# A sparse four-layer graph network on one core: layer 3 gathers only filled slots, shorter clears behind fourth gathers, and layer 2 moved inside the layer 1 loop

## The chip, the cores and the metric

The kernel runs on one core of a Trainium2 chip. The metric is the time of one execution in microseconds on the device. Of several executions the median is given. The trace and its page come from one further execution, taken by the hardware profiler. TensorE is PE in the profile (its weight loads are PEld), VectorE is DVE, ScalarE is ACT, GpSimd is POOL and SyncE is SP.

## The reference

The input is x, 2708 rows of 128 floats, and adj, a 2708 x 2708 matrix. adj has random entries with a density of 0.0059 and a full diagonal, so a row holds some 17 entries, and at most 32. Four layers follow each other, each as `x = layernorm(x + layer(x, adj))`:

```python
# layer 0: mean over the incoming entries
adj.T @ x / adj.sum(axis=0)
# layer 1: messages, an update, its own layer norm
messages = gelu(s[:, None, :] + d[None, :, :] + msg_b)      # s, d: two projections of x
aggregated = einsum('ijd,ij->id', messages, adj)
h = gelu(concat([x, aggregated]) @ upd_w.T + upd_b) + x
# layer 2: batch norm over the rows, leaky ReLU
h = adj @ (x @ W) + b
# layer 3: four heads of attention over the neighbours
s = leaky_relu(x1[:, None, :] + x2[None, :, :], 0.01) @ a    # x1 = x @ w1, x2 = x @ w2
s = exp(tanh(s / 8) * 8) * adj
out = leaky_relu(s / s.sum(-1, keepdims=True) @ x @ Wlin.T, 0.01)
concat(out of the heads) @ w
```

Only pairs (i, j) with an entry in adj matter in layers 1 and 3. The kernel has a sparse path, described here, for inputs whose rows have few enough entries, and a dense one, which this input doesn't take. Arrays named `wrong`, `wrong3` collect whether an input breaks an assumption of the sparse path.

## The kernel before

**Layer 0.** The rows of adj are loaded in 22 blocks of 128 rows. For each block TensorE adds up layer 0's product (L453), GpSimd clears the diagonal (an affine_select, L443), and VectorE extracts the entries of each row, column numbers and values, into lists of 32 slots (`extract`; max8 and find_index, L483 and L478). The nodes are sorted by their number of entries, in two groups: the first 13 blocks and the other 9 (`SPLIT = 13`). Sorted rows lie in 22 new blocks; `QUARTERS` states for every 32 rows of a block how many slots can be filled at most. A tile `caps` holds those limits, written by 88 GpSimd memsets of 32x1 at the start (L415); VectorE uses it in layer 0's checks. After layer 0 the table `d_dram` holds a row d for every node, and `dx_dram` what a node needs for itself.

**Layers 1 and 2** run together. A loop goes over i = 0..21 with the sorted block b = TURNS[i]. `messages` (L919) transposes the block's x into a PSUM tile `own`, computes its term s with two matmuls (the second adds msg_b), and then takes the neighbours in chunks of 5 to 8 slots, 55 chunks in all. For each slot GpSimd gathers up to 128 rows of `d_dram` with one indirect DMA (L263) into a chunk tile `msg`; there are five chunk tiles, used in turn. VectorE adds s (L954), ScalarE applies GELU (L957), VectorE weighs each slot and adds it up (L938). `update` (L964) computes the new x of the block, and SyncE writes it to `x2_dram`, which the profile calls x_dram (digits are left out of names); x2_first and x2_second appear as x_first and x_second. With the last chunks some blocks of layer 3's lists are spread over partitions (`spread`, L669 and L675). Each iteration then also transposes a block of adj's rows (`transposed`, TensorE L1029, ScalarE L1034, SyncE L1036) into `at_dram`.

For layer 2, `layer2(k)` (L1061) gathers 128 whole rows of `at_dram` into `at_rows` (1.4 MB) and multiplies them with x @ W into six PSUM banks (L1076, six matmuls of up to 512 columns). From i = 11 on each iteration calls `layer2` for two values of k at its end. From i = 14 on each iteration also gathers two blocks of the first group's x back in the original order (`x2_first`, 13 gathers).

All gathers of d_dram, t2_dram and x2_dram go through `gather_spaced` (L272). After every fourth gather of a table it clears a tile `pause` of 200 bytes three times (L280), ordered behind the gather; the next gather of that table is ordered behind the last clear.

The order of instructions on each engine in these layers is not written by hand. A scheduler sorts what the program lists, by dependencies and estimated durations. So a change in the program can move instructions far from its own line, on several engines; the built order of each engine is known before any run.

**Between layers 2 and 3** come the batch norm, the masks for the seven kinds of layer 3 blocks (`masks`, L1165: which slot and row a partition stands for), and a table `t2_dram` with a row of 644 floats per node: its projection for four heads (512), its x (128) and four terms of the heads.

**Layer 3** is ordered by hand. The sorted nodes lie in 24 blocks (`BLOCKS3`), each of four quarters of g x j rows. A chunk holds g rows with c = 128 // g slots each on g x c partitions (120 to 128). Four chunks, one of each quarter, make a quad; there are 100 quads. `fetch(i)` (L1635) gathers the four chunks of a quad into a tile `g4` (a pool of `GOT = 9`). `repeated` (L1455) lets TensorE repeat the own terms for the slots (L1463) and add chunks 2 and 3 of g4 (L1469). VectorE adds z to chunks 0 and 1 in place (L1663) and computes leaky ReLU times a for the others (L1664, L1479) and for chunks 0 and 1 (L1487), writing the products into g4 over the gathered projections. ScalarE sums them per head (L1495). `rest` (L1499) takes two quads at a time: tanh, exp, the softmax sum (L1519), and the weighted sum of neighbours with TensorE (L1540), which reads another part of g4. `finish` and the layer norm follow per block, and an indirect DMA scatters finished rows to the output (L284). In the loop the gathers of quad i + 1 are issued at the start of quad i, as far as free tiles allow.

## Time and profile before

| what | value |
|---|---|
| median of 3 runs | 1655.01 us (1653.0 to 1659.47) |
| profiled execution | 1660.39 us, span 1658.7 us |
| mean granted TensorE clock | 0.755 |
| busy share of PE / DVE / ACT / POOL | 70% / 66% / 49% / 63% |
| L263 POOL, gathers of t2_dram (layer 3) | 400, 400.0 us busy, mean 1000 ns |
| L263 POOL, gathers of d_dram (layer 1) | 368, 347.9 us busy, mean 945 ns |
| L280 POOL, clears of pause | 591, 150.5 us busy, mean 255 ns |
| layer 0 / layers 1 and 2 / between / layer 3 and end | 0 to 207 / 207 to 864 / 864 to 959 / 959 to 1659 us |

The span runs from the first to the last instruction of the profiled execution; the difference to its time is what the device needs around it. In lines of the profile `g<-t_dram,idx` names what is written and what is read, `x400` is the number of instructions, and `<-` ahead of an engine or DMA names what ended an idle time. The time that GpSimd is shown in an indirect DMA counts as busy (L263); issuing any other DMA doesn't. "issue" as a releaser means that the engine waited for nothing that the profile shows.

### The profile page before, as it was taken

To read this page: it belongs to the slowest core of one execution; us is meant where nothing else is said; L and a number is where in the kernel's file an instruction comes from. 1 tells how busy PE (TensorE), PEld (TensorE's weight loads), DVE (VectorE), ACT (ScalarE), POOL (GpSimd) and SP (SyncE) were. 2 spreads that over 40 slices of the span, in tenths; PEclk is the share of its full clock that TensorE was granted. 3 is DMA by queue.
4 is the path that set the end of the run, shared out by engine and by line. 5 is a ranking of instruction groups with operands and counts; after the bars stand their busy time and mean duration, and the time that the engine had idled before them with its cause. 6 is when DMAs were issued, how large, how long until landed. Compare 5 with 4: busy or idle time off the path is not lost. (4 is left out here: it accounts for less than half of the span.)

```text
span 1658.7 us, 23258 instructions
## 1 busy us (share of the span) xinstructions
PE 1164.1 (70%) x5179; PEld 735.5 (44%) x5179; DVE 1093.4 (66%) x4560; ACT 811.9 (49%) x3491; POOL 1045.7 (63%) x1656
## 2 busy tenths in 40 slices
PE   7976434566248667353576778988889788898985
PEld 6976323445136433131333324544444445454444
DVE  6999767888435452264465555877768777587874
ACT  2638467755134210021122545776658666576763
POOL 2001487777776626777762577777777777777772
PEclk9998555555555578676566877999889999788996
DMA  8633367879546744811111576777677676676761
GB/s 277 260 135 132 90 171 226 240 213 259 135 103 174 252 172 153 314 52 48 41 42 35 202 204 189 200 212 204 190 202 219 192 199 187 191 208 188 216 190 39
DMA packets 163651, 288.42 MB, mean 174 GB/s; under 512 B 46786, under 2 KB 118514, under 8 KB 156401
## 3 DMA queue, kind: packets, MB, share of 16 engines
q0 software_dynamic: 60208, 189.68, 39.4%
q1 hardware_dynamic: 98053, 93.97, 18.4%
q10 hardware_dynamic: 5240, 3.18, 0.8%
q8 instruction: 44, 0.72, 0.2%
q14 instruction: 106, 0.87, 0.2%
HBM read 241.22 MB, written 45.45 MB: 173 GB/s over the span
## 5 line engine op out<-in xcount | busy, mean ns | idle before, releaser
L263 POOL DMA_INDIRECT g<-t_dram,idx x400 | 400.0, 1000 | 149.0 <-issue 105.7
L263 POOL DMA_INDIRECT msg<-d_dram,idx x368 | 347.9, 945 | 132.6 <-issue 78.7
L1495 ACT ACTIVATE g<-g 126x128 f32<-126x128 f32 (+3 forms) x1200 | 352.9, 297 | 65.7 <-DVE g L1487 25.7
L1469 PE MATMUL z<-g,ident 126*126 126x512 f32 (+3 forms) x400 | 245.4, 734 | 69.6 <-DMA g<-t_dram,idx 60.2
L1495 ACT ACTIVATION_READ_ACCUMULATOR g<-g 126x1 f32 (+3 forms) x1200 | 226.0, 188 | 3.6 <-issue 3.3
L1029 PE MATMUL pt_a<-ident,rows 128*128 128x128 f32 (+2 forms) x475 | 119.5, 411 | 118.8 <-ACT at_sb L1034 62.4
L1469 PEld LDWEIGHTS z<-g,ident 126*126 126x126 f32 (+3 forms) x400 | 73.8, 213 | 229.0 <-DMA g<-t_dram,idx 151.7
L1463 PE MATMUL z<-x,copies 32*126 32x512 f32 (+3 forms) x800 | 160.8, 686 | 7.8 <-DVE g L1663 4.8
L280 POOL MEMSET pause<- 1x200 int8 x591 | 150.5, 255 | 20.7
L453 PE MATMUL acc<-x_nat,rows 128*128 128x129 f32 (+3 forms) x1012 | 132.2, 293 | 30.5 <-DMA rows<-in_adj_dram 19.4
L1029 PEld LDWEIGHTS pt_a<-ident,rows 128*128 128x128 f32 (+2 forms) x475 | 84.4, 210 | 146.8 <-ACT at_sb L1034 76.1
L1663 DVE TENSOR_TENSOR g<-g,z 126x1024 f32<-126x1024 f32 (+3 forms) x100 | 121.7, 1217 | 41.8 <-PE z L1463 21.5
L1076 PE MATMUL acc<-at_rows,x_nat 128*128 128x512 f32 (+2 forms) x264 | 139.4, 676 | 13.4 <-DMA at_rows<-at_dram,perm 13.4
L453 PEld LDWEIGHTS acc<-x_nat,rows 128*128 128x128 f32 (+2 forms) x1012 | 126.1, 202 | 36.2 <-DMA rows<-in_adj_dram 20.7
L1487 DVE SCALAR_TENSOR_TENSOR g<-g,a_ps 126x1024 f32<-126x1024 f32 (+3 forms) x100 | 121.2, 1212 | 0.0
L938 DVE SCALAR_TENSOR_TENSOR own<-msg,ls,own 128x128 f32<-128x128 f32 (+1 forms) x302 | 105.4, 349 | 20.6 <-ACT msg L957 10.5
L957 ACT ACTIVATE msg<-msg 128x896 f32<-128x896 f32 (+4 forms) x55 | 50.4, 916 | 137.7 <-DVE msg L954 68.6
L1479 DVE SCALAR_TENSOR_TENSOR g<-z,a 126x128 f32<-126x128 f32 (+3 forms) x400 | 91.9, 285 | 35.0 <-PE z L1469 31.0
L1540 PEld LDWEIGHTS po_s<-wm,g 126*128 126x128 f32 (+3 forms) x800 | 105.3, 208 | 17.4 <-issue 12.3
L954 DVE TENSOR_TENSOR msg<-msg,own 128x896 f32<-128x896 f32 (+4 forms) x55 | 57.4, 1043 | 79.8 <-DMA msg<-d_dram,idx 76.1
L1540 PE MATMUL po_s<-wm,g 126*128 126x24 f32 (+6 forms) x800 | 103.4, 280 | 1.4 <-DVE wm L1527 0.9
L478 DVE FIND_INDEX8 ci<-cv,rows 128x8 uint32<-128x247 f32 (+2 forms) x242 | 98.5, 407 | 0.0
(319 smaller groups left out, 2058.2 us busy)
## 6 DMA issues: line engine op xcount, KB each, us to landing
rows<-in_adj_dram SPq DMA_DIRECT2D x34, 1354.0 KB
at_dram<-at_sb SPq DMA_DIRECT2D x105, 256.0 KB
t_dram<-t_row SPq DMA_DIRECT2D x10, 644.0 KB
g<-t_dram,idx POOLq DMA_INDIRECT x400
msg<-d_dram,idx POOLq DMA_INDIRECT x368
x_s<-dx_dram SPq DMA_DIRECT2D x21, 128.0 KB
at_dram<-at_sb SPq DMA_DIRECT2D x21, 64.0 KB
x_dram<-x_n SPq DMA_DIRECT2D x21, 64.0 KB
```

Of the source, the lines that this page charges most:

```text
L263: return nc.gpsimd.indirect_dma_start(out=dst, out_offset=None, in_=table[0 : min(N, table.shape[0]), :], in_offset=bass.IndirectOffsetOnA ...
L280: did = nc.gpsimd.memset(pause, 0)
L453: nc.tensor.matmul(accs0[k][0:m, c0 : c0 + f1 - f0], lhsT=rows[0:n, j0 : j0 + m], rhs=x_nat[0:n, b, f0:f1], start=k not in started, stop=( ...
L938: nc.vector.scalar_tensor_tensor(to, m, v, last, ALU.mult, ALU.add)
L1029: nc.tensor.transpose(pt[0:m, j, 0:n], rows[0:n, c0 : c0 + m], ident[0:n, 0:n])
L1076: nc.tensor.matmul(accs2[c][:, 0:cw], lhsT=xw[0:n, b, :], rhs=at[0:n, c0 : c0 + cw], start=(k == 0), stop=(k == NBLK - 1),)
L1463: nc.tensor.matmul(z2[0:e, r, :] if r < 2 else zs[r - 2][0:e], lhsT=copies[g][rows, j, :], rhs=own[b][1][rows, :], start=True, stop=r < 2, ...
L1469: nc.tensor.matmul(zs[r - 2][0:e], lhsT=ident[0:e, 0:e], rhs=g4[0:e, r, 0:HD], start=False, stop=True, skip_group_check=True,)
L1487: nc.vector.scalar_tensor_tensor(z, z, 0.0, a_ps[0:e].unsqueeze(1).to_broadcast((e, 2, HD)), ALU.max, ALU.mult)
L1495: nc.scalar.activation(product, product, AF.Identity, accum_out=sc[0:e, r, hd : hd + 1])
L1540: nc.tensor.matmul(po[:, p0 * HEADS : (p0 + g) * HEADS], lhsT=g4s[i][0:e, r, HD : HD + D], rhs=wm[0:e, 4 * i + r, :, :], start=True, stop= ...
L1663: nc.vector.tensor_tensor(z, z, z2[0:e], ALU.add)
```

## The change

- `gather_spaced` clears `pause` twice after a fourth gather instead of three times (394 clears in all instead of 591).
- Layer 3 lays its slots out slot by slot (c, g) instead of row by row (g, c), so that filled slots come first, and a new table `QUARTERS3` states how many slots a quarter of a block fills. From the ninth quad on a gather fetches only `g * QUARTERS3` rows. The first eight quads fetch all rows, which leaves finite numbers in all eight tiles. Rows gathered in layer 3: 50,460 before, 47,208 after. The new counts are 128 (60 gathers), 126 (61), 120 (70), 119 (32), 117 (21), 115 (16), 114 (40), 112 (36), 110 (32), 108 (9), 105 (5), 104 (3), 100 (3), 96 (6) and 90 (6).
- `GOT` is 8, and the g4 tiles are eight fixed ones. The results of VectorE go to a new tile `made` (two buffers) instead of into g4.
- `masks` builds the mask of a row from an iota over all c x g slots, a comparison and a reduction, instead of from an iota over g.
- `wrong3` has two columns per block; `caps3` and `of_block` serve the new check of the counts.
- The memsets of `caps`, now with those of `caps3`, stand behind the first rows of adj instead of at the start: 126 instead of 88, of them 46 of 128x1 and 80 of 32x1.
- `layer2(k)` is called in `messages`, behind the matmul that adds msg_b (`term`), for two values of k in each iteration from i = 12 on, and one iteration later than before. In the built order of TensorE, k = 5 to 13 stood between the own transposes of iterations 13 and 14 before; after it there are two blocks in each of the iterations 12 to 21.
- `x2_first` is gathered from i = 16 on, three blocks in each iteration. In the built order of GpSimd its first gather stood behind the fourth gather of chunk 34 before, and stands behind the sixth gather of chunk 36 after (chunks counted from 0).

```diff
+QUARTERS3 = [
+    (31, 26, 25, 24), (23, 22, 22, 22), (21, 21, 21, 20), (20, 20, 20, 19),
+    (19, 19, 19, 19), (18, 18, 18, 18), (18, 17, 17, 17), (17, 17, 16, 16),
+    (16, 16, 16, 16), (15, 15, 15, 15), (14, 14, 14, 14), (14, 13, 13, 13),
+    (13, 12, 12, 12), (11, 11, 10, 9), (30, 26, 24, 24), (23, 23, 22, 21),
+    (21, 21, 20, 20), (20, 19, 19, 19), (18, 18, 18, 18), (17, 17, 17, 16),
+    (16, 16, 16, 15), (15, 15, 14, 14), (14, 13, 13, 13), (12, 12, 11, 9),
+]
...
-GOT = 9
+GOT = 8
...
-    wrong3 = keep.tile([P, NB3], FP, name="wrong3")
+    wrong3 = keep.tile([P, 2 * NB3], FP, name="wrong3")
...
-            for _ in range(3):
+            for _ in range(2):
...
-        for b in range(NBLK):
-            for q, most in enumerate(QUARTERS[b]):
-                nc.gpsimd.memset(caps[32 * q : 32 * q + 32, b : b + 1], float(most))
+        caps3 = work.tile([P, NB3], FP, name="caps3")
...
-                part = mine.tile([P, g, c], FP, name=f"spread{g}", tag="spread", bufs=2)
+                part = mine.tile([P, c, g], FP, name=f"spread{g}", tag="spread", bufs=2)
                 nc.vector.tensor_tensor(
                     part,
-                    lists3[:, b % 6, k0 : k0 + c].unsqueeze(1).to_broadcast((P, g, c)),
-                    of_row[g].unsqueeze(2).to_broadcast((P, g, c)),
+                    lists3[:, b % 6, k0 : k0 + c].unsqueeze(2).to_broadcast((P, c, g)),
+                    of_row[g].unsqueeze(1).to_broadcast((P, c, g)),
                     ALU.mult,
                 )
                 nc.tensor.matmul(
                     po[0:e, c0 + i * q : c0 + (i + 1) * q],
-                    lhsT=part.rearrange("p g c -> p (g c)"),
+                    lhsT=part.rearrange("p c g -> p (c g)"),
...
-            n, bad = 4 * g * j, wrong3[:, b : b + 1]
-            nc.vector.tensor_scalar(bad[0:n], node3[0:n, b, 0:1], float(c - 1), None, ALU.is_gt)
+            n = 4 * g * j
+            nc.vector.tensor_scalar(
+                wrong3[0:n, b : b + 1], node3[0:n, b, 0:1], 1.0, None, ALU.is_lt
+            )
             nc.vector.scalar_tensor_tensor(
-                bad[0:n], node3[0:n, b, 0:1], 1.0, bad[0:n], ALU.is_lt, ALU.add
+                wrong3[:, NB3 + b : NB3 + b + 1], lists3[:, b % 6, 2 * SLOTS : 2 * SLOTS + 1],
+                caps3[:, b : b + 1], of_block[g * j], ALU.is_gt, ALU.mult,
...
-        of_row, of_chunk = {}, {}
+        of_row, of_chunk, of_block = {}, {}, {}
+        spans = sorted({g * j for g, j in BLOCKS3})
+        of_blocks3 = work.tile([P, len(spans)], FP, name="of_blocks3")
+        for i, e in enumerate(spans):
+            of_block[e] = of_blocks3[:, i : i + 1]
+            nc.vector.tensor_scalar(of_block[e], in32, float(e), None, ALU.is_lt)
...
+        for b in range(NBLK):
+            for q, most in enumerate(QUARTERS[b]):
+                if not q or most != QUARTERS[b][0]:
+                    at = slice(32 * q, 32 * q + 32) if q else slice(0, P)
+                    nc.gpsimd.memset(caps[at, b : b + 1], float(most))
+        for b in range(NB3):
+            for q, most in enumerate(QUARTERS3[b]):
+                if not q or most != QUARTERS3[b][0]:
+                    at = slice(32 * q, 32 * q + 32) if q else slice(0, P)
+                    nc.gpsimd.memset(caps3[at, b : b + 1], float(most - 1))
...
-        def messages(b, x_s, three):
+        def messages(b, x_s, three, beside):
...
-            nc.tensor.matmul(
+            term = nc.tensor.matmul(
                 s_ps[0:n], lhsT=ones[0:1, 0:n], rhs=msgb[0:1, :], start=False, stop=True
             )
+            for k in beside:
+                with tc.issue_after(term.ins):
+                    layer2(k)
...
-            x_st, agg = messages(b, x_s, three)
+            x_st, agg = messages(
+                b, x_s, three,
+                range(2 * (i - 12), 2 * (i - 11) if i + 1 < NBLK else i) if i > 11 else (),
+            )
...
-            if i >= 11:
-                for k in range(2 * (i - 11), min(i, 2 * (i - 10))):
-                    layer2(k)
-            if i > SPLIT:
-                if i == SPLIT + 1:
+            if i > SPLIT + 2:
+                if i == SPLIT + 3:
                     x2_first = late.tile([P, SPLIT, D], FP, name="x2_first", tag="late")
-                for b in range(2 * (i - SPLIT - 1), min(SPLIT, 2 * (i - SPLIT))):
+                for b in range(3 * (i - SPLIT - 3), min(SPLIT, 3 * (i - SPLIT - 2))):
...
-            nc.gpsimd.iota(row_of, pattern=[[1, g], [0, c]], base=0, channel_multiplier=0)
-            start = small.tile([P, g], I32, name=f"start{g}", tag="start", bufs=2)
-            nc.gpsimd.iota(start, pattern=[[-c, g]], base=0, channel_multiplier=1)
+            nc.gpsimd.iota(row_of, pattern=[[0, c], [1, g]], base=0, channel_multiplier=0)
+            apart = small.tile([P, c, g], I32, name=f"apart{g}", tag="apart", bufs=2)
+            nc.gpsimd.iota(apart, pattern=[[-g, c], [-1, g]], base=0, channel_multiplier=1)
...
-            after = small.tile([P, g], FP, name=f"after{g}", tag="after", bufs=2)
+            here = small.tile([P, c, g], FP, name=f"here{g}", tag="here", bufs=2)
+            nc.vector.tensor_scalar(
+                here.rearrange("p c g -> p (c g)"), apart.rearrange("p c g -> p (c g)"),
+                0.0, None, ALU.is_equal,
+            )
+            mask[g] = ready.tile([P, g], FP, name=f"mask{g}")
+            nc.vector.tensor_reduce(mask[g], here.rearrange("p c g -> p g c"), AX.X, ALU.add)
             count = small.tile([P, 1], FP, name="count", bufs=2)
-            nc.vector.tensor_scalar(
-                after, start, 0.0, None, ALU.is_ge, ALU.add, accum_out=count
-            )
-            mask[g] = ready.tile([P, g], FP, name=f"mask{g}")
             nc.vector.scalar_tensor_tensor(
-                mask[g], start, float(c), after, ALU.is_lt, ALU.mult
+                each, jrow[:, 0:g], 1.0, mask[g], ALU.add, ALU.mult, accum_out=count
...
-        got = layer.enter_context(tc.tile_pool(name="s3_got", bufs=GOT, reuse_waits="tile"))
+        got = layer.enter_context(tc.tile_pool(name="s3_got", bufs=1, reuse_waits="tile"))
...
-        def products(e, g4):
-
-            z = g4[0:e, 0:2, 0:HD]
+        def products(e, made):
+
+            z = made[0:e, 0:2, :]
...
+        sets = [got.tile([P, 4, RW], FP, name=f"g4_{i}") for i in range(GOT)]
+
         def fetch(i):
             b, j = quads[i]
             e = BLOCKS3[b][0] * (P // BLOCKS3[b][0])
-            g4 = got.tile([P, 4, RW], FP, name="g4")
+            g4 = sets[i % GOT]
             for r in range(4):
                 ch = CHUNK3[b] + 4 * j + r
-                gather_spaced(g4[0:e, r, :], t2_dram, idx3[0:e, ch : ch + 1])
+                m = BLOCKS3[b][0] * QUARTERS3[b][r] if i >= GOT else e
+                gather_spaced(g4[0:m, r, :], t2_dram, idx3[0:m, ch : ch + 1])
...
-            z, a_row = g4[0:e, 0:2, 0:HD], a_99.rearrange("p h d -> p (h d)")
-            nc.vector.tensor_tensor(z, z, z2[0:e], ALU.add)
+            made = small.tile([P, 4, HD], FP, name="made", bufs=2)
+            a_row = a_99.rearrange("p h d -> p (h d)")
+            nc.vector.tensor_tensor(made[0:e, 0:2, :], g4[0:e, 0:2, 0:HD], z2[0:e], ALU.add)
             nc.vector.scalar_tensor_tensor(
-                g4[0:e, 2, 0:HD], zs[0][0:e], 0.0, a_row[0:e], ALU.max, ALU.mult
-            )
-            scores(e, 3, zs[1], a_row, g4, sc4[:, 3, :])
+                made[0:e, 2, :], zs[0][0:e], 0.0, a_row[0:e], ALU.max, ALU.mult
+            )
+            scores(e, 3, zs[1], a_row, made, sc4[:, 3, :])
```

## The prediction

> **What bounds the kernel now.** I read the page's engine rows first: no engine is over 70% busy, so the bound changes along the way. The windows view, cut at the stages, says where (columns: stretch, its length, then busy us and instructions of PE, PE's weight loads, DVE, ACT and POOL, the granted clock, the DMA share, GB/s):
>
> ```profile
> 207.00:443.00 236.00, 120.92 (x505) 92.62 (x504) 173.72 (x866) 139.11 (x253) 180.14 (x272) 0.54 0.78 216
> 443.00:592.00 149.00, 81.63 (x292) 59.38 (x292) 69.68 (x355) 45.51 (x116) 104.77 (x156) 0.53 0.63 183
> 592.00:629.00 37.00, 34.57 (x113) 19.46 (x114) 21.66 (x104) 8.07 (x25) 0.87 (x3) 0.85 0.19 69
> 629.00:864.00 235.00, 121.67 (x347) 67.84 (x346) 102.38 (x408) 36.31 (x93) 180.30 (x273) 0.68 0.35 115
> ...
> 959.00:1620.00 661.00, 574.52 (x2583) 308.16 (x2586) 480.82 (x1582) 436.08 (x2672) 493.57 (x716) 0.89 0.71 201
> ```
>
> In four of the five POOL is the busiest or near it, and its idle time there is made of the 0.30 us that follows every gather: 716 instructions in layer 3, 400 of them gathers with 0.30 behind each, fill 661 us. Second, POOL's own timeline. It shows a quad of layer 3, and the one long hole:
>
> ```profile
> 592.35 0.25 POOL L280 MEMSET pause<- 1x200 int8 x1
> 628.74 0.95 POOL L263 DMA_INDIRECT x_first<-x_dram,rank  x1 [36.13 <-issue]
> ...
> 1028.28 1.19 POOL L263 DMA_INDIRECT g<-t_dram,idx  x1 [0.30 <-issue]
> ...
> 1253.24 0.95 POOL L263 DMA_INDIRECT g<-t_dram,idx  x1 [0.30 <-issue]
> ...
> 1337.46 0.88 POOL L280 MEMSET pause<- 1x200 int8 x3
> 1338.94 1.00 POOL L263 DMA_INDIRECT g<-t_dram,idx  x1 [0.60 <-ACT lin_s L1566]
> ```
>
> Four gathers and three clears repeat with no other hole: 99 quad periods from 959.0 to 1615.0, 6.63 us each. The hole at 592.6 is the first gather of x2_first; it needs the rows that update 12 writes, whose write SyncE issued at 626.40. Third, the waits view, for who waits on whom:
>
> ```profile
> PEld z L1469 <- DMA g<-t_dram,idx: 151.7, 116, 4.6
> ...
> POOL x_first L263 <- issue: 38.1, 13, 36.1
> ```
>
> In layer 3 TensorE waits for gathered rows; POOL waits for TensorE only 8.7 + 6.2 us (what released L263 in the groups view). So **POOL bounds layer 3**, and layers 1 and 2 except from 443 to 629. There DVE's add L954 starts 20 to 51 us after its chunk's gathers ended, all five chunk tiles are full, and the chain of DVE, ACT, TensorE and the loads of dx_dram sets the pace.
>
> **Part 1, one clear fewer behind a fourth gather.** Three clears show as 0.88 us, two as 0.57 elsewhere in the timeline: 0.31 less, 100 times in layer 3, **-31 us**. The transfers had it as cover if they need the pause; against that, the first eight quads (128 rows, cheapest) ran at 5.75 us a quad and 224 GB/s without a wait of POOL, faster than the ~6.3 expected here. In layers 1 and 2 there are 97 clears fewer: 30 us of POOL, worth something only where POOL is the bound.
>
> **Part 2, rows of empty slots.** 50,460 rows of layer 3 become 47,208. Rows are not what POOL pays for: by the timeline a 128-row gather takes 0.947, 126 rows 0.984, 120 rows 0.980, 125 rows 1.197; in layer 1, 96 rows 0.932 and 32 rows 0.882. After the change 102 gathers have a count that 16 divides, 224 another even count, 74 an odd one. By the rows nearest: 102 x 0.947 + 224 x 0.982 + 74 x 1.197 = 405 us, against 400.0 now: **+5**. Bounds for the 209 gathers whose count has no row in layer 3: all at 0.932 gives -18, all at 1.197 gives +37. What the rows save lies in the DMA engines (71% busy, not the bound), so I count nothing for it.
>
> The 125-row gather costs 0.21 more than the 126-row one, though it moves less. The Trainium skill, page "DMA: Bandwidth & Descriptors", section "Why a DMA increments its semaphore by 16 and not by 1", has a rule for it: a DMA uses the largest number of engines up to 16 that divides the row count. That speaks against this change, since 128 rows use 16 engines, but 119 use 7, 117 use 13, 115 use 5 and 114 use 6. A line through the 126- and 125-row durations (9 against 25 rows per engine) makes the sum +2.5 instead of +5 by this estimate; 115 and 119 rows would then be the dear ones, 117 would not, and the time 1583.
>
> The g4 tiles are 8 instead of 9 and results go to `made`. In the built order the first gather of a quad mostly waits for 2 or 3 semaphores instead of 4; behind a clear the gap is 0.60 with four and 0.445 with two, so some 0.1 x 90 quads: **-8**. One tile fewer costs nothing while TensorE is at most 22 us (3.5 quads) behind POOL, as in quads 3 to 13; if it falls further, up to +6 once.
>
> Layer 3: -31 + 5 - 8 = **-34**, so 6.3 us a quad. Next in line is TensorE: 574.5 us busy in 100 quads, 5.75 each, plus weight loads that don't overlap. It has some 70 us of waits for landings to give. I take -32.
>
> **Part 3, the order in layers 1 and 2.** In the built order the first x2_first gather stands behind the sixth gather of chunk 36, instead of the fourth of chunk 34. From 592.6 POOL then goes on: three gathers of chunk 34, chunk 35 (its tile is free after chunk 30, added at 584.1), chunk 36 (tile of chunk 31, added at 600.6), and three or four at_rows. At 1.25 a gather, 0.57 for the clears and 1.4 for at_rows that is about 26 us of work that now stands behind the hole; some 10 us of hole are left. Behind 629, 37 groups lose 0.31: -11; two at_rows more fall there: +2.5. The thirteen x2_first gathers still all come before the end. Sum **-34**.
>
> Upstream, 207 to 443 is POOL-bound and loses 35 x 0.31 = 11 us. Also 88 clears of caps (3.14 to 14.41 us) leave the start, where DVE waits 11.42 us for POOL; 126 clears come back behind the first affine_select, so extract(1) comes at about 28 instead of 31: -3. But the stretch 443 to 629 is bound by the other chain, with loads that don't come sooner for it. Bounds 0 and -14; I take **-7**.
>
> The layer2(k) blocks (4.79 us of TensorE each at 600 to 640) now stand two per iteration behind the term matmul, where nine of them stood between the transposes of iterations 13 and 14. There chunk 37 was added 28.8 us after its gathers: that stall goes. Beside them DVE and ACT work on three chunks (1.04 + 0.92 + 7 x 0.35 us each, some 13), which covers 9.6 us. One block more can stand ahead of the last update, and masks add up to 0.5 us per kind on DVE: **+3** in the tail.
>
> Sum: -32 - 34 - 7 + 3 = **-70** from the profiled 1660.4 (span 1658.7). The median of the runs shown is 1655.0, 5.4 less; I take the difference from it: 1585, rounded to **1586**.
>
> **Rivals.**
> *TensorE becomes the bound in layer 3.* For: in quads 72 to 82, at a clock near 0.8, it paced the loop at 6.57 us. Against: 151.7 us of weight-load waits for gathers. Then layer 3 gives 99 x (6.63 - 6.57) = -6, and the total is -44: **1611**.
> *The other engines bound layer 1 to the end.* For: from 443 to 629 they do. Against: chunks 41 to 47 were added 1.6 to 2 us after their gathers. Then that part gives -10 in place of -38: **1613**.
> *Uneven counts are dear.* All unseen counts at 1.197: layer 3 gives -2, **1616**. This is also the case where the rows don't help at all.
> *The pause was needed.* The gathers then wait for the DMA engines what the clears took: only the hole pays, -26: **1629**. Against it: 5.75 us at 224 GB/s.
> *Slower: layer2 blocks hold the update.* Two blocks between the term matmul and the update put TensorE in each iteration from 12 to 21. At a clock of 0.5, as granted from 207 to 592, a block is some 7.2 to 8 us, and if its at_rows has not landed (a gather of 1.4 MB that shares the DMA engines with the chunks) it waits as well. The shortest iteration seen, add 600.6 to add 614.4, is 14 us; with two blocks and a landing each it could reach 33. It decides from about 30 us per iteration, since POOL's own pace is 25. Ten iterations of 33 are 330 against 274 us now (594 to 868), +56, less 31 in layer 3: **1680**. Against: the clock was 0.68 to 0.85 behind 592, and at_rows are gathered one to two iterations ahead.
>
> **How the numbers follow.** Forecast 0.48 (own range 1560 to 1606), TensorE-bound layer 3 0.15, other engines in layer 1 0.15, dear counts 0.05, pause needed 0.07, three of these together (about 1650) 0.04, slower 0.06. Low end: gathers at 0.932 (-18 - 5 from 1586) and no hole left; high end: it reaches to the pause case. Range 1557 to 1630. A measurement here can tell 0.5% (8.3 us) from no change: faster 0.90, same 0.04, slower 0.06.
>
> **What would show it.** Right: POOL's quad period near 6.3 with x2 clears; no POOL hole over 15 us between 580 and 660; x2_first behind chunk 36; waits of z L1469 for gathers halved; layer 3 some 630 us long. Wrong: gaps of POOL in layer 3 released by PE or ACT (GOT, TensorE); 117-row gathers at 1.2 us (no matter of divisors) or 114-row ones too; DVE add lags of 20 us and more behind chunk 40; TensorE waiting for at_rows in L1076. The prediction fails most if the clock granted in layer 3 drops, since TensorE is next there.

## The result, and the profile after

The changed kernel takes 1707.93 us (median of 4 runs, 1704.63 to 1714.6), the kernel before 1654.12: ratio 1.0321, 95% interval 1.0287 to 1.0355. It is 3.2% slower; 1586 was predicted. The profiled execution took 1714.6 us, its span is 1712.9. In what follows, "before" and "after" are the two profiled kernels, and line numbers are those of the kernel after (before's L263, L280, L938, L954, L1469 are L271, L288, L965, L981, L1498).

Some of the costliest groups on GpSimd and VectorE of after (busy us, mean ns of one, then idle time before them):

```profile
L271 POOL DMA_INDIRECT g<-t_dram,idx x400 | 403.1, 1008 | 166.9 <-issue 87.8
L271 POOL DMA_INDIRECT msg<-d_dram,idx x368 | 347.2, 943 | 182.2 <-issue 84.8
...
L965 DVE SCALAR_TENSOR_TENSOR own<-msg,ls,own 128x128 f32<-128x128 f32 (+1 forms) x302 | 105.6, 350 | 75.8 <-remote 24.9
...
L288 POOL MEMSET pause<- 1x200 int8 x394 | 100.2, 254 | 9.7
```

What the change set out to do on GpSimd happened: 197 clears fewer, 50 us of busy time gone, and the gathers cost what they cost before. So the loss isn't in the busy time of GpSimd's instructions. The windows of after, cut where before's were cut (length, then busy us and count of PE, PEld, DVE, ACT, POOL, granted clock, DMA share, GB/s), and the first of them in before:

```profile
207.00:300.00 93.00, 19.25 (x76) 13.55 (x75) 40.29 (x172) 38.80 (x59) 67.08 (x95) 0.52 0.47 128
300.00:443.00 143.00, 70.42 (x280) 54.93 (x280) 101.17 (x509) 75.71 (x141) 89.53 (x122) 0.57 0.73 208
443.00:592.00 149.00, 84.37 (x352) 65.17 (x352) 89.66 (x457) 60.79 (x148) 84.28 (x117) 0.55 0.59 156
...
1010.00:1680.00 670.00, 596.51 (x2600) 318.51 (x2600) 484.14 (x1600) 439.23 (x2696) 473.46 (x620) 0.87 0.69 186
```

```profile
207.00:300.00 93.00, 39.27 (x176) 29.89 (x176) 69.14 (x331) 67.88 (x109) 72.92 (x111) 0.56 0.73 205
```

In the first 93 us after layer 0, PE, DVE and ACT did some half of their former work, though GpSimd issued as many gathers (62 of d_dram, 61 before), and the DMA share fell from 0.73 to 0.47. Something held all three at once while the transfers had room. A table of when each part begins (us from the start of the span) shows where the 54 us came from:

| | chunk 10 added | chunk 20 | chunk 33 | chunk 36 | chunk 54 | first gather of layer 3 | end |
|---|---|---|---|---|---|---|---|
| before | 335 | 443 | 614 | 670 | 868 | 959.0 | 1658.7 |
| after | 366 | 492 | 648 | 671 | 908 | 1009.7 | 1712.9 |

Layers 1 and 2 lose 31 us by chunk 10 and 49 by chunk 20, gain 33 back at the hole of x2_first (chunks 33 to 36), and lose 40 more behind it. From the first gather of layer 3 to the end it is 699.7 us before and 703.2 after: layer 3 gave nothing. Its 99 quad periods did get shorter, 645.1 us in place of 656.0, but from the last quad's first gather to the end it is 58.1 us in place of 43.7.

**What the loss looks like.** VectorE's own timeline in after, from the fourth chunk (the bracket is the idle time before an instruction and what ended it):

```profile
244.65 0.34 DVE L965 SCALAR_TENSOR_TENSOR own<-msg,ls,own 128x128 f32<-128x128 f32 x1
244.90 0.41 DVE L489 MAX8 cv<-rows 128x8 f32<-128x247 f32 x1
252.64 0.35 DVE L965 SCALAR_TENSOR_TENSOR own<-msg,ls,own 128x128 f32<-128x128 f32 x1 [7.33 <-issue]
252.91 0.08 DVE L484 MATCH_VALUE_LOAD ci<-cv,rows 128x8 f32 x1
252.98 0.41 DVE L484 FIND_INDEX8 ci<-cv,rows 128x8 uint32<-128x247 f32 x1
255.44 0.35 DVE L965 SCALAR_TENSOR_TENSOR own<-msg,ls,own 128x128 f32<-128x128 f32 x1 [2.06 <-remote]
255.71 0.41 DVE L489 MAX8 cv<-rows 128x8 f32<-128x247 f32 x1
259.64 0.36 DVE L965 SCALAR_TENSOR_TENSOR own<-msg,ls,own 128x128 f32<-128x128 f32 x1 [3.52 <-remote]
```

The L965 at 252.64 adds a slot to the sum that the L965 at 244.65 wrote. That one ended at 244.99 and the max8 behind it at 245.31; the next 7.33 us are empty, and the view names no releaser ("issue"). A semaphore is a counter that an engine or a DMA raises when it is done, and others wait for its value. The instruction at 252.64 waits for one semaphore only, VectorE's own. So the news of VectorE's own result came late. The same line in the kernel with three clears (run after_3clears below), at the same place:

```profile
242.60 0.34 DVE L965 SCALAR_TENSOR_TENSOR own<-msg,ls,own 128x128 f32<-128x128 f32 x1
242.85 0.41 DVE L489 MAX8 cv<-rows 128x8 f32<-128x247 f32 x1
243.18 0.34 DVE L965 SCALAR_TENSOR_TENSOR own<-msg,ls,own 128x128 f32<-128x128 f32 x1
```

Between engines it is the same. ScalarE's timeline of after has one step of an update waiting 16.56 us for a product of TensorE, which in TensorE's timeline had ended at about 791.2:

```profile
805.22 0.28 ACT L1011 ACTIVATE new<-tail 128x128 f32<-128x128 f32 x1 [16.56 <-remote]
```

```profile
790.41 0.80 PE L1006 MATMUL tail<-u_t,agg_t 128*128 128x128 f32 x2
```

The trace also records updates of semaphores. In after from 249 us (time in us / number of the semaphore; 108 belongs to PE, 109 to DVE, 110 to ACT, 99 to POOL, 111 to 118 to DMAs):

```
249.43/110 249.91/110 250.60/108 251.23/109 252.08/99 252.40/99 253.30/113
254.01/113 254.71/115 255.42/109 256.10/116 256.90/118 257.22/111 257.51/99
```

Fourteen recorded updates of every kind in 9 us, mostly some 0.70 us apart, as if one place dealt with them one at a time; after_3clears has 73 in the same 9 us. The record isn't complete: of the 3035 updates that VectorE's instructions make in after it holds 2088. So 0.70 us is the spacing of recorded updates; the empty 7.33 us stand in the instructions' own times. GpSimd meanwhile goes on issuing gathers, six of them in these 9 us. I call such a time a **late stretch**. Two measures of it come from the trace: the sum of DVE's gaps over 0.9 us that only wait for DVE itself ("own waits"), and the sum of 5 us slices in which most updates are over 0.45 us apart ("late time"). Before has 9.9 us of own waits and 70 us of late time, after 61.9 and 150. Own waits are the firmer measure. Late time depends on how updates that come in bursts are counted: with each recorded update by itself the same slices give 35 us for before and 95 for after. So it only tells much from little.

So the theory to test: **gathers that follow each other too closely make semaphore updates of all engines late.** In the first 20 us of layer 1, four gathers of 128 rows and their clears take 5.74 us with three clears and 5.42 with two. Rivals: the moved order (part 3) did it, or the fewer rows (part 2), or the scheduler's different built order for two clears; and, for layer 3, that GpSimd, TensorE or ScalarE bounds it.

### The profile page after: what moved, and what is told of

The parts are those of the page before. It is cut to its first block, busy times and chain, and to the rows that moved or that the text cites. A ratio compares the mean times of both kernels' runs of the same rounds, so it can differ in the third digit from the quotient of the medians.

```text
span 1712.9 us, 23072 instructions
## 1 busy us (share of the span) xinstructions
PE 1181.2 (69%) x5179; PEld 744.7 (43%) x5179; DVE 1098.3 (64%) x4575; ACT 811.2 (47%) x3491; POOL 1001.7 (58%) x1497
## 5 line engine op out<-in xcount | busy, mean ns | idle before, releaser
L271 POOL DMA_INDIRECT g<-t_dram,idx x400 | 403.1, 1008 | 166.9 <-issue 87.8
L271 POOL DMA_INDIRECT msg<-d_dram,idx x368 | 347.2, 943 | 182.2 <-issue 84.8
L1524 ACT ACTIVATE made<-made 126x128 f32<-126x128 f32 (+3 forms) x1200 | 353.0, 297 | 74.6 <-issue 32.2
L1498 PE MATMUL z<-g,ident 126*126 126x512 f32 (+3 forms) x400 | 231.6, 706 | 3.1 <-DMA g<-t_dram,idx 1.5
L1524 ACT ACTIVATION_READ_ACCUMULATOR made<-made 126x1 f32 (+3 forms) x1200 | 226.0, 188 | 2.0 <-issue 1.9
L1492 PE MATMUL z<-x,copies 32*126 32x512 f32 (+3 forms) x800 | 188.3, 714 | 31.2 <-issue 21.7
L1696 DVE TENSOR_TENSOR made<-g,z 126x1024 f32<-126x1024 f32 (+3 forms) x100 | 121.7, 1217 | 56.0 <-remote 20.3
L965 DVE SCALAR_TENSOR_TENSOR own<-msg,ls,own 128x128 f32<-128x128 f32 (+1 forms) x302 | 105.6, 350 | 75.8 <-remote 24.9
L1498 PEld LDWEIGHTS z<-g,ident 126*126 126x126 f32 (+3 forms) x400 | 77.1, 215 | 154.0 <-issue 134.0
L1103 PE MATMUL acc<-at_rows,x_nat 128*128 128x512 f32 (+2 forms) x264 | 132.1, 657 | 0.0
L1516 DVE SCALAR_TENSOR_TENSOR made<-made,a_ps 126x1024 f32<-126x1024 f32 (+3 forms) x100 | 121.2, 1212 | 0.0
L1569 PEld LDWEIGHTS po_s<-wm,g 126*128 126x128 f32 (+3 forms) x800 | 104.4, 207 | 19.6 <-issue 13.8
L288 POOL MEMSET pause<- 1x200 int8 x394 | 100.2, 254 | 9.7
L1508 DVE SCALAR_TENSOR_TENSOR made<-z,a 126x128 f32<-126x128 f32 (+3 forms) x400 | 91.7, 284 | 16.2 <-PE z L1498 10.8
L1492 PEld LDWEIGHTS z<-x,copies 32*126 32x126 f32 (+3 forms) x800 | 57.7, 199 | 91.1 <-issue 54.1
```

Source lines behind the costliest of these rows:

```text
L271: return nc.gpsimd.indirect_dma_start(out=dst, out_offset=None, in_=table[0 : min(N, table.shape[0]), :], in_offset=bass.IndirectOffsetOnA ...
L288: did = nc.gpsimd.memset(pause, 0)
L965: nc.vector.scalar_tensor_tensor(to, m, v, last, ALU.mult, ALU.add)
L1103: nc.tensor.matmul(accs2[c][:, 0:cw], lhsT=xw[0:n, b, :], rhs=at[0:n, c0 : c0 + cw], start=(k == 0), stop=(k == NBLK - 1),)
L1492: nc.tensor.matmul(z2[0:e, r, :] if r < 2 else zs[r - 2][0:e], lhsT=copies[g][rows, j, :], rhs=own[b][1][rows, :], start=True, stop=r < 2, ...
L1498: nc.tensor.matmul(zs[r - 2][0:e], lhsT=ident[0:e, 0:e], rhs=g4[0:e, r, 0:HD], start=False, stop=True, skip_group_check=True,)
```

## The experiments

**Which part does it.** The kernel before with one clear less, the changed kernel with the third clear back, and the changed kernel without part 3 and without part 2's fewer rows.

```diff
# before_2clears (kernel before)        # after_3clears (changed kernel)
-            for _ in range(3):         -            for _ in range(2):
+            for _ in range(2):         +            for _ in range(3):
# after_old_order
+            if i >= 11:
+                for k in range(2 * (i - 11), min(i, 2 * (i - 10))):
+                    layer2(k)
-                for b in range(3 * (i - SPLIT - 3), min(SPLIT, 3 * (i - SPLIT - 2))):
+                for b in range(2 * (i - SPLIT - 1), min(SPLIT, 2 * (i - SPLIT))):
# after_all_rows
-                m = BLOCKS3[b][0] * QUARTERS3[b][r] if i >= GOT else e
+                m = e
```

> The kernel before with two clears behind a fourth gather in place of three, and nothing else. Two theories. A, the clears: in the trace of the changed kernel, semaphore updates of all engines come one at a time, 0.70 us apart, in stretches of 10 to 60 us (some 150 us in all, 70 us before); if denser gathers of GpSimd bring these stretches, this kernel has more of them than the one before, layers 1 and 2 (first gather of layer 3 at 959 us before) become 20 to 50 us longer, and the total is 1675 to 1705. B, the order: the 50 us come from the moved layer2 blocks, the moved x2_first gathers and the moved memsets; then this kernel gains on layers 1 and 2 (10 to 20 us, GpSimd is the bound in parts of them) and the total is 1610 to 1650. In layer 3 (700 us from its first gather to the end): if GpSimd is the bound, 670; if TensorE takes over at once, 690 to 705.

> The changed kernel with three clears again, everything else as changed. Theory A (too few clears slow the semaphores): the 50 us upstream of layer 3 come back, and the hole ahead of x2_first is still gone, so 1630 to 1660. Theory B (the order costs the 50 us): 1700 to 1740, layer 3 starts at 1010 us or later. Layer 3 itself: if TensorE is its bound in the changed kernel, it stays at 700 us or shortens, because GpSimd at 6.6 us a quad is no slower than TensorE; if GpSimd still bounded it, 30 us longer.

> The changed kernel with the calls of layer2 and the gathers of x2_first back at their old places in the program; two clears, layer 3 and the memsets as changed. Theory A: still slow, 1690 to 1730, since the loss sits ahead of chunk 20 and at two clears. Theory B: layer 3 starts near 950 us and the total is 1640 to 1660. Layer 3 700 us under both.

> The changed kernel, but every gather of layer 3 fetches the rows of empty slots too (counts 120 to 128 as before). Layers 1 and 2 are as in the changed kernel (layer 3 starts near 1010). If the rows left out don't matter because TensorE bounds layer 3: within 6 us of the changed kernel. If uneven counts cost GpSimd time that decides: 10 to 30 us faster. If fewer rows did help: 10 us and more slower.

| run | median, us | ratio to before, interval | own waits / late time, us | first gather of layer 3 | layer 3 |
|---|---|---|---|---|---|
| before_2clears | 1736.21 | 1.0485, 1.0449 to 1.0522 | 61.2 / 155 | 1032.6 | 706.3 |
| after_3clears | 1648.58 | 0.9954, 0.9934 to 0.9973 | 4.2 / 40 | 952.4 | 696.6 |
| after_old_order | 1732.32 | 1.0465, 1.0443 to 1.0488 | 63.8 / 130 | 1033.6 | 698.4 |
| after_all_rows | 1723.84 | 1.0421, 1.0372 to 1.0470 | 61.0 / 125 | 1002.9 | 713.8 |

("Layer 3" here and below is from its first gather to the end.) One number in the kernel before, 3 to 2, costs 4.85%; the same number put back in the changed kernel takes 3.6% off (0.9954 against 1.0321). Part 1 is the loss; the order and the rows each help a little beside it. The windows of after_3clears show DVE, ACT, PE and the DMA share of the first 93 us back near before's:

```profile
207.00:300.00 93.00, 38.10 (x152) 28.03 (x152) 68.14 (x318) 68.42 (x105) 72.28 (x113) 0.56 0.73 202
```

**Pace, or what else a clear does.**

```diff
# after_2x300, after_2x320
-    pause = keep.tile([1, 200], I8, name="pause")
+    pause = keep.tile([1, 300], I8, name="pause")      # or 320
# after_1x300_each: the 300 bytes, and
-        if count_of[table.name] % 4 == 0:
-            for _ in range(2):
+        if True:
+            for _ in range(1):
# after_3then2
-            for _ in range(2):
+            for _ in range(2 if table.name == t2_dram.name else 3):
```

> The changed kernel with two clears of 300 bytes. By the rows 200 bytes take 0.255 us and a clear some 0.84 ns per byte more, so four gathers with their clears take some 5.59 us, between the changed kernel's 5.42 and the 5.74 of three clears. The built order is nearly that of the changed kernel (21 rows of VectorE's differ, against 663 from the order with three clears). Theory A, the rate of GpSimd's gathers decides: about the same time as the kernel with two clears of 320 bytes (within 15 us), somewhere in 1645 to 1700, with slow stretches of the semaphores shorter than in the changed kernel. Theory O, the built order that the scheduler makes from the clears decides: 1700 to 1715, as the changed kernel.

> Two clears of 320 bytes: four gathers take some 5.62 us, but the built order is nearly that of three clears (34 rows of VectorE's differ, against 678 from the changed kernel). Theory A: about as with 300 bytes, within 15 us. Theory O: 1640 to 1655, as with three clears, and 50 us faster than with 300 bytes.

> The changed kernel with one clear of 300 bytes behind every gather instead of two of 200 behind every fourth: by the rows 0.95 + 0.34 + 0.16 = 1.45 us a gather, evenly, against 1.355 in the changed kernel and 1.435 with three clears. If the mean rate of gathers is what slows the semaphores: no slow stretch at 230 to 300 us, 1640 to 1665. If a long gap behind every fourth gather is needed (something has to run empty): slow as the changed kernel or slower, 1700 to 1760.

> The changed kernel with three clears in layers 1 and 2 and two in layer 3 (the gathers of t2_dram). Upstream it should be as with three clears everywhere (layer 3 starts near 952). Layer 3 took 696.6 us with three clears and 703.2 with two. If two clears slow layer 3 by themselves: 700 to 710 and a total of 1650 to 1662. If only what came before slowed it, and TensorE bounds it: 685 to 697, total 1638 to 1650. If GpSimd still bounded it: 665 to 675, total 1617 to 1628.

| run | four gathers, us | median, us | ratio, interval | own waits / late time | first gather of layer 3 | layer 3 |
|---|---|---|---|---|---|---|
| after_2x300 | 5.58 | 1694.58 | 1.0229, 1.0186 to 1.0272 | 45.0 / 150 | 1008.8 | 688.6 |
| after_2x320 | 5.63 | 1672.93 | 1.0147, 1.0103 to 1.0191 | 46.0 / 130 | 979.1 | 684.2 |
| after_1x300_each | 5.79 | 1647.08 | 0.9950, 0.9928 to 0.9971 | 23.1 / 75 | 953.2 | 692.7 |
| after_3then2 | 5.75 | 1647.50 | 0.9975, 0.9959 to 0.9991 | 4.0 / 65 | 940.5 | 702.1 |

The number of clears is not what matters: two long ones are better than two short ones, one behind every gather as good as three behind every fourth. after_3then2 splits the places: with three clears in layers 1 and 2 the upstream loss is gone, but two clears in layer 3 gain nothing there (702.1 against 696.6 in after_3clears). At 5.58 and 5.63 the first own waits come at some 255 us instead of 232.

Pace and order are mixed between after_2x300 and after_2x320, which have different built orders. They are not mixed between after_2x320 and after_3then2, and this pair carries the argument: both ran on one chip, and up to 575 us their traces have the same instructions in the same order on TensorE, VectorE, ScalarE and GpSimd, the clears aside. Four gathers take 5.63 us in one and 5.75 in the other. By 570 us the own waits are 31.3 us and 4.0, and chunk 20 is added at 472 and 436 us. From 250 to 330 us, after_2x320 and then after_3then2:

```profile
250.00:330.00 80.00, 28.23 (x108) 21.83 (x109) 45.38 (x204) 40.45 (x65) 57.62 (x78) 0.50 0.57 168
```

```profile
250.00:330.00 80.00, 44.78 (x178) 34.30 (x178) 68.13 (x347) 59.74 (x102) 60.83 (x93) 0.54 0.80 232
```

With the slower issue PE and DVE do half as much again in the same time, and the DMA share rises from 0.57 to 0.80.

**Rows, order, and TensorE in layer 3.**

```diff
# after_half_rows (changed kernel, layer 1)
-                    m = filled(b, c0 + k)
+                    m = min(filled(b, c0 + k), 64)
# after_old_order_3clears: after_old_order with range(3)
# after_3then2x300: after_3then2, layer 3's two clears of 300 bytes
# after_3then2_less_pe: after_3then2, and
-                    start=True, stop=r < 2, skip_group_check=r >= 2,
-                )
-            for r in (2, 3):
-                nc.tensor.matmul(
-                    zs[r - 2][0:e], lhsT=ident[0:e, 0:e], rhs=g4[0:e, r, 0:HD],
-                    start=False, stop=True, skip_group_check=True,
+                    start=True, stop=True, skip_group_check=r >= 2,
```

> The changed kernel (two clears), but a gather of layer 1 fetches at most 64 rows (the other half of a chunk tile keeps old numbers, so the messages are not those of the reference). Number of gathers, their order and the built order of VectorE are those of the changed kernel; by the rows a gather takes 0.917 instead of 0.945 us. Theory C, the count of gathers per time slows the semaphores: the stretch at 230 to 296 us and the one near 690 stay, 1690 to 1715. Theory R, the rows or bytes that they move do it: the stretches go and the total is 1630 to 1665.

> The changed kernel with the calls of layer2 and the gathers of x2_first at their old places, and three clears. What the new order is worth at three clears: my sum gave it some 24 us (34 without the 10 for the clears). If so, layer 3 starts near 976 and the total is 1668 to 1675. If the hole of 36 us ahead of x2_first only returns in another wait, or the new order gives it back behind the last chunk (from the iota of jrow to layer 3 it was 86 us in place of 71): 1645 to 1658.

> Three clears of 200 bytes in layers 1 and 2, two of 300 in layer 3 (5.6 us instead of 5.42 or 5.74 for four gathers of 128 rows). Layer 3 took 688.6 us at two of 300, 684.2 at two of 320, 696.6 at three of 200, 702 and 703 at two of 200, but in kernels with other things ahead of it. If layer 3 has its best pace there by itself: 684 to 690, total 1627 to 1642, faster than both kernels. If those lengths came from what was ahead: 695 to 703, total 1643 to 1652.

> Three clears in layers 1 and 2, two in layer 3, and TensorE's two matmuls with the unit matrix per quad left out in layer 3 (the gathered rows of chunks 2 and 3 are not added; 734 ns twice, with their weight loads some 2.4 us of TensorE per quad). With the matmuls, layer 3 took 702 us. Theory T, TensorE bounds layer 3 at two clears: it shrinks to GpSimd's pace, 6.2 to 6.4 a quad, 655 to 675 in all, total 1605 to 1622. Theory S, the slow semaphore updates at two clears bound it whatever TensorE has to do: 690 to 705, total 1640 to 1650.

| run | median, us | ratio, interval | own waits / late time | first gather of layer 3 | layer 3 |
|---|---|---|---|---|---|
| after_half_rows | 1755.54 | 1.0553, 1.0504 to 1.0601 | 88.5 / 205 | 1029.1 | 724.2 |
| after_old_order_3clears | 1660.57 | 0.9976, 0.9952 to 1.0000 | 12.9 / 110 | 959.0 | 696.3 |
| after_3then2x300 | 1673.57 | 1.0035, 0.9998 to 1.0072 | 12.8 / 65 | 964.7 | 698.2 |
| after_3then2_less_pe | 1674.23 | 1.0055, 1.0027 to 1.0083 | 15.1 / 100 | 964.0 | 702.8 |

after_half_rows moves fewer bytes in layer 1, has VectorE's instructions in the same order as after, and is slower still, with more own waits: a short gather is issued sooner (four in 5.24 us). It ran on another chip, and its layer 3, which is that of after, took 21 us longer as well, so the size of the step isn't clean. But half the rows and bytes don't take the late stretches away: they go with the number of gathers in a time, and need no full DMA engines:

```profile
207.00:300.00 93.00, 19.62 (x79) 13.88 (x78) 43.28 (x183) 41.33 (x64) 65.04 (x95) 0.53 0.41 112
```

after_old_order_3clears against after_3clears (0.9976 and 0.9954) makes part 3 worth about 0.2% with three clears; the intervals overlap, so it isn't shown to be worth anything there. after_3then2x300 has clears of 300 bytes in layer 3 alone, and layer 3 takes 698.2 us, not the 688.6 and 684.2 of the kernels with long clears everywhere: what comes ahead of layer 3 has its part in those, or the chip (9 here, 2 there). after_3then2_less_pe leaves out two of TensorE's six products for z per quad, and layer 3 is as long as in after_3then2 (702.8 and 702.1). The windows of it and of after_3then2, over the same time, say why:

```profile
1010.00:1580.00 570.00, 495.17 (x1947) 317.18 (x1947) 420.84 (x1407) 387.27 (x2397) 413.47 (x538) 0.56 0.71 189
```

```profile
1010.00:1580.00 570.00, 515.43 (x2331) 283.02 (x2330) 428.33 (x1416) 386.34 (x2385) 418.05 (x544) 0.89 0.70 192
```

A sixth fewer matmuls, but busy time falls only 4%, because the granted clock falls from 0.89 to 0.56. TensorE's clock took the work back, so this run could not tell whether TensorE bounds layer 3. The Trainium skill, page "TensorE: Matmul & The Clock Gate", section "Part 1: The HAM clock gate", has the clock follow how busy TensorE has recently been; this run agrees in direction, 0.89 to 0.56.

**More space, even space, and ScalarE.**

```diff
# after_4clears (changed kernel)
-            for _ in range(2):
+            for _ in range(4):
# after_1x352_each: as after_1x300_each, with 352 bytes
# after_3clears_all_rows: after_3clears with m = e
# after_3then2_less_act: after_3then2, and
-            sums_of_products(e, made, sc4, (0, 1))
+            nc.scalar.copy(sc4[0:e, 0:2, :], made[0:e, 0:2, 0:HEADS])
```

> The changed kernel with four clears of 200 bytes behind a fourth gather: by the rows 6.05 us for four gathers of 128 rows, against 5.42 at two (ratio to the kernel before 1.032) and 5.74 at three (0.995). If the slow stretches still cost time at three clears: ratio 0.975 to 0.99. If three clears are already free of them and GpSimd's own pace counts: 100 x 0.31 in layer 3 and some of 97 x 0.31 ahead of it, ratio 1.01 to 1.03.

> The changed kernel with one clear of 352 bytes behind every gather: 1.49 us a gather instead of 1.45 at 300 bytes (ratio 0.995) and 1.435 with three clears behind a fourth (0.995). If the best pace is reached at 1.435 to 1.45: ratio 1.00 to 1.015, since GpSimd's time comes on top. If slow stretches still cost there: 0.985 to 0.995.

> The changed kernel with three clears, and with the rows of empty slots fetched in layer 3: what leaving the rows out is worth where the semaphores are not slowed. Ratio with them left out 0.995. My sum: gathers 5 us cheaper with all rows, so 0.992. If fewer rows do help (less traffic beside the loads of own rows): 0.998 to 1.005.

> Three clears in layers 1 and 2 and two in layer 3 (ratio 0.9975), and ScalarE's eight sums over the products of chunks 0 and 1 left out of every quad of layer 3: one copy of four columns stands in their place, so the scores are not those of the reference, and ScalarE has 3.7 us less per quad. Theory T, TensorE with the clock it is granted paces layer 3 at two clears: layer 3 shortens by less than 10 us, ratio 0.99 to 1.00. Theory V, the chain of VectorE and ScalarE behind TensorE paces it: layer 3 comes to GpSimd's 6.3 a quad, 25 us and more shorter, ratio 0.97 to 0.985.

| run | four gathers, us | median, us | ratio, interval | own waits / late time | first gather of layer 3 | layer 3 |
|---|---|---|---|---|---|---|
| after_4clears | 6.06 | 1702.82 | 1.0194, 1.0141 to 1.0248 | 4.3 / 30 | 971.8 | 729.9 |
| after_1x352_each | 5.96 | 1630.18 | 0.9763, 0.9711 to 0.9815 | 9.3 / 35 | 930.4 | 698.2 |
| after_3clears_all_rows | 5.74 | 1665.25 | 0.9982, 0.9953 to 1.0012 | 27.6 / 70 | 968.9 | 693.6 |
| after_3then2_less_act | 5.74 | 1677.93 | 1.0048, 1.0019 to 1.0077 | 22.7 / 100 | 974.1 | 703.0 |

A fourth clear brings nothing upstream (971.8 against 968.9 in after_3clears_all_rows, on the same chip) and costs some 33 us in layer 3: beyond some pace more space only costs. With ScalarE's work in the window 1010 to 1580 cut from 386 to 187 us busy, layer 3 is 703.0 against 702.1: ScalarE is not its bound. after_1x352_each beats both kernels. The fewer rows at three clears are inside the error (0.9982 and 0.9954).

The chip has a part of its own. Six kernels have three clears and the same instructions in the same order up to layer 3, and ran on four chips:

| chip (by the kernel before, us) | run | first gather of layer 3 | own waits |
|---|---|---|---|
| 2 (1653.13) | after_3then2 | 940.5 | 4.0 |
| 14 (1654.33) | after_3clears | 952.4 | 4.2 |
| 9 (1665.6) | after_3then2_less_pe, after_3then2x300 | 964.0, 964.7 | 15.1, 12.8 |
| 8 (1669.54) | after_3clears_all_rows, after_3then2_less_act | 968.9, 974.1 | 27.6, 22.7 |

On one chip they are some 5 us apart at most, between chips up to 34 apart. So small differences between runs on different chips say little here.

**Pace at one built order, on two chips.** Two clears of 320, 352 and 384 bytes give the same built order on TensorE, ScalarE and SyncE, and on VectorE all but some 60 lines of difference. So the pace differs, and the chip: after_2x320 ran on chip 2, the other two on chip 12.

```diff
# after_2x352, after_2x384 (changed kernel)
-    pause = keep.tile([1, 200], I8, name="pause")
+    pause = keep.tile([1, 352], I8, name="pause")      # or 384
```

> The changed kernel with two clears of 352 bytes in place of two of 200, again with the built order of two clears of 320 bytes (54 lines apart on VectorE). Two clears take 0.76 us, so four gathers come in about 5.68 us. If the pace alone decides: between the runs with 320 and 384 bytes, ratio 0.995 to 1.013, with a slow stretch that begins later than 255 us or none. If the built order decides: ratio 1.010 to 1.020 and a slow stretch from about 255 us.

> The changed kernel with two clears of 384 bytes in place of two of 200. Its built order is that of the run with two clears of 320 bytes on TensorE, ScalarE and SyncE, and 60 lines apart on VectorE; only the pace of the gathers differs. By the slope between clears of 200 bytes (254 ns) and 352 bytes (382 ns) two of them take some 0.82 us, three of 200 bytes 0.85, so four gathers come in about 5.73 us instead of 5.63. If the pace alone decides: the stretch from 255 us with one semaphore update per 0.70 us is gone or short, VectorE's waits on its own results fall from 46 us to under 15, ratio 0.990 to 1.005. If the built order decides: waits stay at 40 us or more, ratio 1.010 to 1.020.

| run | four gathers, us | median, us | ratio, interval | own waits / late time | first gather of layer 3 | layer 3 |
|---|---|---|---|---|---|---|
| after_2x320 (above) | 5.63 | 1672.93 | 1.0147, 1.0103 to 1.0191 | 46.0 / 130 | 979.1 | 684.2 |
| after_2x352 | 5.67 | 1584.22 | 0.9654, 0.9625 to 0.9684 | 0 / 0 | 899.8 | 681.1 |
| after_2x384 | 5.75 | 1591.13 | 0.9691, 0.9660 to 0.9722 | 0 / 0 | 906.1 | 684.6 |

The late stretches are gone, and both theories had expected less. after_2x352 is the best version of all, 4.9 points below after_2x320. From 250 to 330 us it has:

```profile
250.00:330.00 80.00, 44.49 (x178) 33.51 (x178) 68.90 (x352) 59.64 (x102) 62.58 (x83) 0.59 0.88 242
```

With the slightly slower issue GpSimd issues 55 gathers of d_dram in these 80 us, 51 in after_2x320, since chunk tiles come free sooner, and the DMA engines reach 0.88.

But that 0.04 us per four gathers did all this is not shown, since chip 12 is unlike the others. Its kernel before is the fastest (1642.06), and its traces record nearly every update: 3005 of VectorE's 3018 in after_2x352, where every trace of the other chips holds at most some seven tenths. That is so from the start: from 20 to 200 us, ahead of the first gathers of layer 1, after_2x320 has 1552 recorded updates and after_2x352 has 2185. So its late time of 0 can't be compared with that of the others; its own waits of 0 can. The kernels before and after were not traced on chip 12, nor was after_2x320 run there. What carries the pace is the pair on chip 2 above.

Pace isn't everything. after_2x384 and after_3clears have the same pace (5.75 and 5.74) and are at 0.9691 and 0.9954. Their chips differ, and so does GpSimd's order behind 560 us. How the 46 us between them upstream divide is open. On chip 2 one clear behind every gather (5.79) has 23.1 us of own waits where after_3then2 (5.75) has 4.0, so the mean pace alone doesn't decide.

## Why the prediction was wrong, point by point

**The step that failed** is part 1's cover: "The transfers had it as cover if they need the pause; against that, the first eight quads (128 rows, cheapest) ran at 5.75 us a quad and 224 GB/s without a wait of POOL". It asked whether the gathers need the pause, looked at POOL's waits and the bandwidth, and found nothing. Both readings were true and beside the point: in the first late stretch of after, up to 300 us, GpSimd's gathers have one gap over 0.7 us (1.24), and the DMA engines are at 0.47. The others need the pause, to hear of each other's results. And 5.75 us a quad lay just on the good side: on one chip and in one order, 5.75 has 4.0 us of own waits and 5.63 has 31.3 by 570 us. The rival "The pause was needed" named the right cause with the wrong victim (gathers that wait for DMA), hence 1629 and a chance of 0.07; no case had layers 1 and 2 slower through part 1. The trace of before has a hint of it: late stretches from 415 to 440 and from 670 to 695 us, and 9.9 us of own waits from 428 to 453.

**Upstream, 207 to 443: -11 at most, and -7 taken for all of 0 to 629.** Measured +49 by chunk 20 (492 in place of 443). It is the same failed step: "POOL-bound" was read from busy time and from GpSimd's gaps, and a faster GpSimd then made its consumers slower.

**Layer 3: predicted -32, measured +3.5.** The waits look like the rival "TensorE becomes the bound in layer 3" (1611), but no run shows that TensorE's own work is the cause. The waits view of after, then of after_3clears and of after_2x352 (in all, times, longest):

```profile
POOL g L271 <- PE po_s L1569: 40.5, 41, 10.0
...
PEld z L1498 <- DMA g<-t_dram,idx: 19.9, 29, 3.0
```

```profile
PEld z L1498 <- DMA g<-t_dram,idx: 125.3, 93, 3.6
```

```profile
PEld z L1498 <- DMA g<-t_dram,idx: 195.7, 151, 4.6
...
POOL g L271 <- PE po_s L1569: 17.7, 51, 0.5
```

In after TensorE hardly waits for rows, GpSimd waits for TensorE to free tiles (10.0 us in one piece at the ninth quad), and the end of a quad's L1498 lies 11 to 20 us behind its gathers in half of the quads, 29.8 at most (before: 4.7 to 7.3, and 22.5). "It has some 70 us of waits for landings to give" was the right reserve to look at, and it was not enough. A quad takes 6.52 us in after (6.63 before) and 6.41 in after_2x352, where TensorE lags 4 to 9 us and still waits 195.7 us for rows. The median quad fell from 6.33 to 6.10 us, 0.23 of the 0.33 that was taken; the rest went in waits for tiles and behind the last quad. So with two short clears GpSimd's pace alone is not the bound any more, and the best layer 3 (681.1 us) comes with clears that are longer than the change made them, on chip 12. Nine g4 tiles would not have saved it: before_2clears has nine, and its layer 3 takes 706.3 us. Why TensorE takes longer in after, 596.5 us for 2600 matmuls at a clock of 0.87 against 474.6 for 2299 at 0.91 in after_2x352, isn't settled: it lags from quads 3 to 7 on, where a late stretch lies (1045 to 1050 us), and the run that took work off TensorE was answered by its clock.

**Gather sum: predicted 405, measured 403.1.** Right, with bounds far too wide, and by luck: wrong prices that evened out. The durations by row count in after (median ns):

| rows | 128 | 126 | 120 | 119 | 117 | 115 | 114 | 112 | 110 | 105 |
|---|---|---|---|---|---|---|---|---|---|---|
| ns | 946 | 986 | 980 | 1091 | 992 | 1181 | 1117 | 944 | 996 | 955 |

"Another even count" at 0.982 and "an odd one" at 1.197 is wrong: 114 is dear, 117 and 105 are cheap. The Trainium skill, page "DMA: Bandwidth & Descriptors", section "Why a DMA increments its semaphore by 16 and not by 1", lets a DMA use the largest number of engines up to 16 that divides the rows. The prediction's estimate by that rule, +2.5, is nearer to the measured +3.1 than its own +5. These durations agree with the rule throughout: 119 on 7 engines, 115 on 5 and 114 on 6 have 17, 23 and 19 rows each and are the three dear ones; 117 on 13 and 105 on 15 have 9 and 7. The fewer rows gave 1.0 point with two clears (1.0421 to 1.0321) and nothing measurable with three.

**Fewer semaphores behind a clear, -8.** The median idle time ahead of a quad's first gather fell from 0.59 to 0.52 us, 0.07 of the 0.1 that was taken.

**Part 3: predicted -34, of it -26 at the hole.** The table gives 56 us from chunk 33 to 36 before and 23 after: -33, of it 19.6 at the first gather of x2_first alone. The timeline of after:

```profile
649.16 0.25 POOL L288 MEMSET pause<- 1x200 int8 x1
665.97 0.96 POOL L271 DMA_INDIRECT x_first<-x_dram,rank  x1 [16.55 <-DMA x_dram<-x_n]
```

The hole went from 36.1 to 16.6 us instead of to 10, and is 6.7 in after_2x352, which has no own waits. But a hole that closes pays only if what follows keeps up: from chunk 36 to 54 after loses 39 us again, where the prediction had a gain (-8.5 from 629 us on). With three clears the whole of part 3 is worth 0.2%, inside the error.

**The start, -3; the tail, +3.** The first gather of layer 1 comes at 203.4 instead of 211.2 us: -7.8, right in sign. From the first iota of the masks to layer 3's first gather it is 70.6 us before and 86.4 after: +16. With the old order it is 78.8, which puts some 8 of it down to the new masks and the rest to the order.

**The slower rival, layer2 blocks (1680, 0.06).** Not it: with layer2 at its old place the kernel is slower still (1732.32).

**Readings that were off.** "Its idle time there is made of the 0.30 us that follows every gather" holds for 96 of the 167 us that GpSimd is idle in before's window 959 to 1620; wider gaps ahead of a quad's first gather are another 42. The same row has TensorE busier than GpSimd there, 574.52 against 493.57 us. By the prediction's own prices the bounds of the unseen counts are -20 and +36 in place of -18 and +37, and its low end is 1553, since its terms are -23 and -10 from 1586; neither decides anything.

In all, on chip 12, where no own waits are seen, the terms of the sum come near: after_2x352 makes all the edits but shortens the pause by less, and takes 1584.22 us where the kernel before takes 1642.06, -58 us of the -70 that were predicted. How those 58 us divide isn't known, as before was not traced there.

## What to carry to other kernels

An instruction that does nothing useful can set the pace of another stream; before it is shortened, ask who profits from the pause, and look at all engines, not only at the one that pauses and the transfers it issues. Where an instruction that only waits for its own engine's last result starts microseconds late, or where several engines slow down together while the DMA share falls, read the semaphore updates: if they come one at a time, space out the stream that issues most DMAs, and try several spaces, since 0.03 us more per gather moved chunk 20 of this kernel from 472 to 436 us. Compare on one chip, since the same code was up to 34 us apart upstream between chips. A busy share says nothing about what a faster engine does to the others.

## What the runs showed of the hardware

- With indirect DMAs issued one after the other from GpSimd at 1.41 us each (four in 5.63), engines heard of results late, their own too: 31.3 us of own waits by 570 us, against 4.0 at 1.44 us each (four in 5.75), on one chip and in one order. In such a time the trace records updates of PE, DVE, ACT, GpSimd and DMAs about 0.70 us apart. It isn't a sharp threshold for every place or chip: before (1.435) has 9.9 us of own waits, one 300-byte clear behind each gather (1.45) 23.1, and the same code with three clears 4.0 to 27.6 on four chips. What it is that serves the updates one by one was not shown. It comes with gathers of 64 rows as well (88.5 us). The profiler doesn't make it: runs without it are as slow (1704.63 to 1708.72 beside 1714.6).
- The Trainium skill, page "DMA: Bandwidth & Descriptors", section "Anatomy of one DMA — SWDGE (gpsimd) path", puts the update of a DMA's semaphore, once the write is confirmed, at some 100 ns. No run here shows that step by itself. What after shows is that in a late stretch recorded updates come about 0.70 us apart, and that an engine sat idle up to 16.56 us, until 14.0 us after the product it waited for.
- A matmul stream that lost a sixth of its matmuls kept its length: the granted clock went from 0.89 to 0.56.
